# Pairs of 64-column stationaries in one attention head of a float32 kernel

## The chip, the cores and the metric

The kernel runs on one core of one Trainium2 chip. The metric is the device time of one execution in microseconds (us); less is better. Engines carry the names of the profile: PE is the matrix engine (PEld is its loading of stationary operands, which has a row of its own), DVE the vector engine, ACT the scalar engine, POOL the GpSimd engine, SP the engine that mostly issues transfers.

## The reference

The input is one sequence of 2048 rows of 256 numbers, all float32. It is normalized, and the same normalized rows go into an attention with 16 heads of 128 and into a feed-forward part with quantized weights; both results are added to the input.

```python
xn = _layernorm(x)                                  # x: (1, 2048, 256)
q, k, v = split(einsum('bsd,ed->bse', xn, Wqkv))    # 16 heads of 128
logits = einsum('bqhd,bkhd->bhqk', q, k) * 128 ** -0.5
w = softmax(logits, axis=-1)
out = einsum('bhqk,bkhd->bqhd', w, v)               # (1, 2048, 16 * 128)
attn = einsum('bse,de->bsd', out, Wout)
ffn = bitlinear(sigmoid(bitlinear(xn, w1)) * bitlinear(xn, w2), w3)
return x + attn + ffn
```

## The kernel before, in words

After a start of about 110 us (normalization, the first head's q, k and v, the feed-forward part) the kernel goes through the attention head by head. A head's 2048 query rows are four blocks of 512 (`b` 0 to 3), and all 64 blocks are numbered through: block `n` is head `n // 4`, so head 2 is blocks 8 to 11. A block is four steps (`t` 0 to 3) of 128 queries. The order of instructions is written out by hand (`tc.manual_schedule()`): each engine takes them in the order in which the main loop records them. The loop runs over steps `u`, and in each step it records, for PE,

- `scores(v)` for a step six ahead (`v = u + LEAD`): the logits of 128 queries against all 2048 keys, as two tiles `s` of 128 queries by 1024 keys, four matmuls in all. A matmul's stationary operand is a 128 x 128 piece of `qT`, its moving operand 512 columns of `kT`. DVE takes each tile's row maximum (line 617), ACT the exponential (line 627).
- one or two products for the next head's q, k and v, or for the output projection (`pw` line 166, `pvw` line 280, `pow` line 783), placed before and among the weighted sums.
- four calls of `weighted(n, k)` (line 690), `k` being one of 16 groups of 128 keys: the stationary operand is a 128 x 128 piece of `v`, the moving operand the 512 columns of the turned exponentials `pT`, and the sum over `k` grows in one tile `av` (128 x 512). After `k` 15 DVE multiplies it by the reciprocal sums (line 701).

Between the two, `exchanged(v)` sends the exponentials through 16 transfers (line 646, queues of SP and ACT) into `part`, and `transposed` (line 680, DVE) turns them in pieces of 32 x 32 into `pT`. So keys reach PE as the summed dimension without a product on PE.

A float32 `matmul` of the program is two passes on PE: the profile shows two loads of the stationary operand and two MATMUL records for each. A record writes its operands as `128*128`, the rows and columns of the array that it uses, and the shape of the moving operand.

Which array columns a matmul uses follows from the program: a stationary operand of 64 columns uses half of them, and which half is set by the partitions of its output, 0 to 63 or 64 to 127.

The loop's body, where the pieces are put in order, is this:

```python
if more:
    scores(v, late=beside)          # `beside` records the first product
...
if u >= 0:
    for k in range(t * KQ, t * KQ + ahead):
        weighted(n, k)
if twice:
    pms.append(product(*hi, True))  # the second product
...
if u >= 0:
    for k in range(t * KQ + ahead, (t + 1) * KQ):
        weighted(n, k)
```

Of the kernel before, what the change touches and what calls it, by code (L numbers as in the profile page):

```python
# [19 lines left out]
def layernorm_attention_bitffn_kernel(  # L20
# [14 lines left out]
    nc = tc.nc  # L35
    P = 128
# [6 lines left out]
    QB = 512  # L43
    NB = S // QB
    TB = QB // P
    NKT = S // P
    KQ = NKT // TB
    HALF = S // 2
# [45 lines left out]
    kTs, qTs, vs = {}, {}, {}  # L94
# [142 lines left out]
    def v_tile(h: int):  # L237

        if h == 1:
            return osums.rearrange("p b e (k d) -> p (b e k) d", d=D)  # L240
        if h not in vs:
            vs[h] = kvpool.tile([P, NKT, D], F32, tag="v", name=f"v{h}", bufs=3)
        return vs[h]

    def v_place(h: int, k: int):


        return (k + NKT // 2) % NKT if h == 1 else k
# [344 lines left out]

    NQ = P // 32
    SP_DMAS = 10

    blocks = [(h, b) for h in range(H) for b in range(NB)]
    sums, exps, parts, pTs, avs, rbs = {}, {}, {}, {}, {}, {}

    def scores(v: int, late=None):  # L600

        n, t = divmod(v, TB)
        h, b = blocks[n]
        halves, ps = [], []
        mx = small.tile([P, 2], F32, tag="mx", name=f"mx{v}")
        for i in range(2):
            s = ps_s.tile([P, HALF], F32, tag="s", name=f"s{v}_{i}")  # L610
            for j in range(HALF // QB):
                nc.tensor.matmul(  # L612
                    s[:, bass.ts(j, QB)], qTs[h, b][:, bass.ts(t, P)],
                    kTs[h][:, i * HALF + j * QB : i * HALF + (j + 1) * QB],
                    start=True, stop=True,
                )
            nc.vector.tensor_reduce(mx[:, i : i + 1], s, AX.X, ALU.max)  # L617
            halves.append(s)
        nm = small.tile([P, 1], F32, tag="nm", name=f"nm{v}")
        nc.vector.tensor_reduce(nm, mx, AX.X, ALU.max, negate=True)  # L620
        if t == 0:
            sums[n] = small.tile([P, TB, 2], F32, tag="sum", name=f"sum{n}")
        if late:
            late()
        for i, s in enumerate(halves):
            p = ppool.tile([P, HALF], F32, tag="p", name=f"p{v}_{i}", bufs=4)
            nc.scalar.activation(  # L627
                p, s, AF.Exp, bias=nm, accum_out=sums[n][:, t, i : i + 1],
            )
            ps.append(p)  # L630
        exps[v] = ps

    def exchanged(v: int):
# [7 lines left out]
        for m, (j, g) in enumerate(todo):  # L641
            queue = nc.sync if m < SP_DMAS else nc.scalar
            if v > len(blocks) * TB - 3:
# [38 lines left out]
    def weighted(n: int, k: int, part=None):  # L682

        h, b = blocks[n]
        t0, t1 = (0, TB) if part is None else (part * TB // 2, (part + 1) * TB // 2)
        if k == 0:
            pool, tag = (ps_s, "s") if part == 0 else (ps_av, "av")
            avs[n] = pool.tile([P, QB], F32, tag=tag, name=f"av{n}_{t0}")
        av = avs[n][:, : (t1 - t0) * P]
        nc.tensor.matmul(  # L690
            av, v_tile(h)[:, v_place(h, k), :],
            pTs[n][:, t0:t1].rearrange("p t g (k q) -> p (t g) k q", q=32)[:, :, k, :],
            start=(k == 0), stop=(k == NKT - 1),
        )
        if k == NKT - 1:

            m = 1 if part == 1 else t1 - t0
            for t in range(t0, t1, m):
                o, a = oT[:, t * P : (t + m) * P], av[:, (t - t0) * P : (t - t0 + m) * P]
                if n < NBK - NB:  # L700
                    nc.vector.tensor_tensor(o, a, rbs[n][:, t * P : (t + m) * P], ALU.mult)  # L701
                else:
                    nc.vector.tensor_copy(o, a)
# [228 lines left out]
    with tc.manual_schedule():  # L932
        for u in range(-LEAD, (NBK - 1) * TB):
            n, t = divmod(u, TB)
# [3 lines left out]
            h, b = blocks[v // TB] if more else (H, 0)  # L938
# [7 lines left out]
            g, i = divmod(n, GB)  # L946
            if n >= NB and t < 2:
                i, j = divmod(i, NB)
                j = 2 * j + t
# [17 lines left out]
            if more:  # L967
                scores(v, late=beside)
# [28 lines left out]
# [3 lines that stand above are left out]
# [13 lines left out]
# [3 lines that stand above are left out]
# [10 lines left out]
        n = NBK - 1  # L1026
        for k in range(NKT):
            weighted(n, k, 0)
            if k in (KQ - 1, 3 * KQ - 1):
                projected(n - 1, k // (2 * KQ), ps_s, "s")  # L1030
            elif k == 2 * KQ - 1:
                opened(NB - 1, 0, ps_s, "s")
# [44 lines left out]
```

## Time and profile before

| what | value |
|---|---|
| time, median of 3 runs | 2243.17 us (2242.22 to 2247.93) |
| profiled execution, from first to last instruction | 2242.2 us |
| the same execution's time outside that span | not given; its span lies within 0.1 us of the fastest run's time |
| granted PE clock, whole span | 1.000 |
| PE busy | 2230.5 us, 5434 passes |
| DVE, ACT, POOL busy | 1772.0, 652.4, 681.1 us |
| scores (line 612) | 2048 passes, 922.5 us busy |
| weighted sums (line 690) | 2080 passes, 947.9 us busy in two groups |

The page gives busy time per engine over the span, and groups of instructions by line, operand names and shape, each with its count, busy time and the mean duration of one. A pass's duration in the records is longer than the distance to the next one, since a pass starts before the one ahead of it has left the array; the distance from start to start says what a pass costs in a row of passes. The time line lists instructions in order: start and length in us, engine, line, operation, and in brackets how long the engine was idle before and what ended that.

### The profile page before, as it was taken

What the parts mean: (1) busy time and instruction counts of PE and PEld (TensorE: products, weight loads), DVE (VectorE), ACT (ScalarE), POOL (GpSimd) and SP (SyncE); (2) the same over time, 40 slices, a digit from 0 to 9 for tenths busy, and PEclk for the clock granted to TensorE, in tenths of its full rate; (3) what the DMA queues carried; (4) which work ended last, traced back from release to release, by engine and by line L of the source; (5) the groups of instructions that cost most, each with busy time, mean ns of one, the idle gap of its engine ahead of it and who ended that gap; (6) DMA issues with size and microseconds to landing.
All of it is one profiled execution on the core that took longest, in us unless ns stands there. A gap on an engine that the chain in (4) does not pass through costs nothing.

```text
span 2242.2 us, 24572 instructions
## 1 busy us (share of the span) xinstructions
PE 2230.5 (99%) x5434; PEld 1025.3 (46%) x5434; DVE 1772.0 (79%) x2329; ACT 652.4 (29%) x1138; POOL 681.1 (30%) x1223
## 2 busy tenths in 40 slices
PE   9999999999999999999999999999999999999999
PEld 6744444444444444444444444444444444444445
DVE  6577778888788878888788878788778887888876
ACT  5543222222222222222222222222222222222231
POOL 0021144231452223522234313332134221452442
PEclk9999999999999999999999999999999999999999
DMA  2166666775676666676666766667566676676775
GB/s 91 50 161 172 156 166 172 186 195 157 165 196 179 185 159 164 188 203 169 155 176 179 197 179 150 176 181 199 163 166 179 175 197 159 158 200 181 197 202 145
DMA packets 252515, 382.72 MB, mean 171 GB/s; under 512 B 86224, under 2 KB 90768, under 8 KB 252368
## 3 DMA queue, kind: packets, MB, share of 16 engines
q1 hardware_dynamic: 127664, 174.95, 30.3%
q10 hardware_dynamic: 74896, 101.94, 17.2%
q0 software_dynamic: 49808, 104.27, 16.6%
q8 instruction: 43, 0.70, 0.1%
q14 instruction: 104, 0.85, 0.1%
HBM read 62.98 MB, written 34.73 MB: 44 GB/s over the span
## 4 chain that ended last, share of the span: by engine, by line
PE 67%; DMA 16%; DVE 7%; SPq 5%; issue 2%; ACTq 2%; ACT 1%; DVEq 0%; POOL 0%
PE s L612 26%; PE av L690 25%; DMA part<-p 16%; PE pw L166 5%; SPq L646 5%; DVE pT L680 3%; PE pvw L280 3%; PE pow L783 3%; PE ph L495 2%; ACTq L646 2%; DVE mx L617 1%; PE pf L518 1%; ACT p L627 1%; DVE osums L790 1%; PE pv L229 1%
## 5 line engine op out<-in xcount | busy, mean ns | idle before, releaser
L627 ACT ACTIVATE p<-s,nm 128x1024 f32<-128x1024 f32 x512 | 566.1, 1110 | 1512.5 <-DMA part<-p 1269.5
L612 PE MATMUL s<-kT,qT 128*128 128x512 f32 x2048 | 922.5, 593 | 2.6 <-ACT p L627 2.4
L617 DVE TENSOR_REDUCE mx<-s 128x1 f32<-128x1024 f32 x512 | 623.6, 1221 | 353.5 <-PE s L612 353.3
L690 PE MATMUL av<-pT,v 128*128 128x512 f32 (+1 forms) x1952 | 888.4, 585 | 0.0
L680 DVE STREAM_TRANSPOSE pT<-part 128x1024 f32<-128x1024 f32 x512 | 605.2, 1220 | 37.3 <-DMA part<-p 31.1
L612 PEld LDWEIGHTS s<-kT,qT 128*128 128x128 f32 x2048 | 388.3, 190 | 493.6 <-issue 474.7
L690 PEld LDWEIGHTS av<-pT,v 128*128 128x128 f32 x1952 | 370.9, 190 | 450.2 <-issue 448.0
L665 POOL DMA_DIRECT2D rd<-r x240 | 124.9, 527 | 616.8 <-DVE r L663 614.0
L311 POOL DMA_DIRECT2D xnT<-v x448 | 221.1, 501 | 84.9 <-DVE v L304 54.4
L723 POOL TENSOR_TENSOR o<-o 128x512 f32<-128x512 f32 x56 | 71.2, 1271 | 198.6 <-PE pow L783 168.4
L708 POOL DMA_DIRECT2D od<-oT x60 | 34.1, 568 | 300.5 <-DVE oT L701 300.5
L790 DVE TENSOR_TENSOR osums<-pow,osums 128x512 f32<-128x512 f32 x196 | 124.2, 675 | 0.0
L627 ACT ACTIVATION_READ_ACCUMULATOR p<-s,nm 128x1 f32 x512 | 100.3, 196 | 0.0
L166 PE MATMUL pw<-t,ws 128*128 128x512 f32 x168 | 86.6, 597 | 1.0 <-DVE kT L193 1.0
L189 DVE TENSOR_TENSOR kT<-pw,kT 128x512 f32<-128x512 f32 x112 | 74.7, 667 | 0.0
L304 DVE TENSOR_TENSOR v<-pvw,v 128x512 f32<-128x512 f32 x98 | 65.5, 680 | 0.1
L690 PE MATMUL av<-pT,osums 128*128 128x512 f32 x128 | 59.5, 592 | 0.0
L186 DVE SCALAR_TENSOR_TENSOR qT<-pw,qT 128x512 f32<-128x512 f32 x84 | 57.5, 684 | 0.1
L166 PE MATMUL pw<-xnT,wk 128*128 128x512 f32 x112 | 57.2, 592 | 0.0
L783 PE MATMUL pow<-o,wos 128*128 128x512 f32 x112 | 57.2, 592 | 0.0
L166 PEld LDWEIGHTS pw<-t,ws 128*128 128x128 f32 x168 | 31.0, 189 | 44.1 <-issue 34.0
L620 DVE TENSOR_REDUCE nm<-mx 128x1 f32<-128x2 f32 x256 | 39.7, 155 | 13.4
(140 smaller groups left out, 1146.6 us busy)
## 6 DMA issues: line engine op xcount, KB each, us to landing
part<-p SPq DMA_DIRECT2D x2556, 64.0 KB, 2.2
part<-p ACTq DMA_DIRECT2D x1540, 64.0 KB, 2.5
oT<-rd POOLq DMA_DIRECT2D x60, 256.0 KB, 4.1
od<-oT POOLq DMA_DIRECT2D x60, 256.0 KB, 3.3
o<-od POOLq DMA_DIRECT2D x60, 256.0 KB, 4.5
xnT<-v POOLq DMA_DIRECT2D x448, 32.0 KB, 2.4
osums<-yd POOLq DMA_DIRECT2D x28, 512.0 KB, 5.4
yd<-osums POOLq DMA_DIRECT2D x28, 512.0 KB, 4.7
```

The source lines that it names most:

```text
L166: nc.tensor.matmul(pm, lhs, rhs, start=True, stop=True)
L189: nc.vector.tensor_tensor(k, pk, base, ALU.add)
L311: nc.gpsimd.dma_start(v_part[q // 2][bass.ts(j, 32), bass.ts(q % 2, S // 8)], v[bass.ts(q, 32), bass.ts(j, S // 8)],)
L612: nc.tensor.matmul(s[:, bass.ts(j, QB)], qTs[h, b][:, bass.ts(t, P)], kTs[h][:, i * HALF + j * QB : i * HALF + (j + 1) * QB], start=True, ...
L617: nc.vector.tensor_reduce(mx[:, i : i + 1], s, AX.X, ALU.max)
L627: nc.scalar.activation(p, s, AF.Exp, bias=nm, accum_out=sums[n][:, t, i : i + 1],)
L646: queue.dma_start(parts[v][g // 2][bass.ts(j, 32), g % 2, :], ps[j // 2][bass.ts(g, 32), bass.ts(j % 2, S // NQ)],)
L665: nc.gpsimd.dma_start(rds[n % 2][:, bass.ts(j, 32)], riT[32 * j : 32 * j + TB, :])
L680: nc.vector.transpose(pTs[n][:, t, 2 * i : 2 * i + 2], part)
L690: nc.tensor.matmul(av, v_tile(h)[:, v_place(h, k), :], pTs[n][:, t0:t1].rearrange("p t g (k q) -> p (t g) k q", q=32)[:, :, k, :], start=( ...
L783: nc.tensor.matmul(pm, lhs, o3[:, i], start=True, stop=True)
L790: nc.vector.tensor_tensor(y, pm, y, ALU.add)
```

## The change

In head 2 every weighted sum is done with stationary operands of 64 columns instead of 128, in pairs: one works on the left half of the array's columns and writes partitions 0 to 63 of `av`, the other on the right half and writes partitions 64 to 127. In blocks 8 and 10 (`b` 0 and 2) both of a pair go over the same 512 moving columns. In blocks 9 and 11 (`b` 1 and 3) each matmul is cut again into two of 256 moving columns, recorded in the order left half with columns 0 to 255, right half with 256 to 511, left with 256 to 511, right with 0 to 255. In blocks 10 and 11 the scores are made in pairs in the same way, each of 64 queries against 512 keys. What is computed, the tiles and all other engines' instructions stay the same, and so does the order of the work around it; all other heads are untouched.

```diff
+    HALVED = 2
...
             for j in range(HALF // QB):
-                nc.tensor.matmul(
-                    s[:, bass.ts(j, QB)], qTs[h, b][:, bass.ts(t, P)],
-                    kTs[h][:, i * HALF + j * QB : i * HALF + (j + 1) * QB],
-                    start=True, stop=True,
-                )
+                m = P // 2 if h == HALVED and b > 1 else P
+                for a in range(0, P, m):
+                    nc.tensor.matmul(
+                        s[a : a + m, bass.ts(j, QB)], qTs[h, b][:, t * P + a : t * P + a + m],
+                        kTs[h][:, i * HALF + j * QB : i * HALF + (j + 1) * QB],
+                        start=True, stop=True,
+                    )
...
-        nc.tensor.matmul(
-            av, v_tile(h)[:, v_place(h, k), :],
-            pTs[n][:, t0:t1].rearrange("p t g (k q) -> p (t g) k q", q=32)[:, :, k, :],
-            start=(k == 0), stop=(k == NKT - 1),
-        )
+        vk = v_tile(h)[:, v_place(h, k), :]
+        pk = pTs[n][:, t0:t1].rearrange("p t g (k q) -> p (t g) k q", q=32)[:, :, k, :]
+        if h == HALVED:
+            m, w = P // 2, QB // (1 + b % 2)
+            for i in range(QB // w):
+                for j in range(2):
+                    q = i ^ (j if w < QB else 0)
+                    nc.tensor.matmul(
+                        av[j * m : (j + 1) * m, bass.ts(q, w)], vk[:, bass.ts(j, m)],
+                        pk[:, q * w // 32 : (q + 1) * w // 32],
+                        start=(k == 0 and i == 0), stop=(k == NKT - 1), skip_group_check=True,
+                    )
+        else:
+            nc.tensor.matmul(av, vk, pk, start=(k == 0), stop=(k == NKT - 1))
```

## The prediction, made before the changed kernel was run

> **What bounds the kernel now.** I first read the page's busy times and slices: PE is busy through all 40 slices at the full granted clock.
>
> ```profile
> PE 2230.5 (99%) x5434; PEld 1025.3 (46%) x5434; DVE 1772.0 (79%) x2329; ACT 652.4 (29%) x1138; POOL 681.1 (30%) x1223
> PE   9999999999999999999999999999999999999999
> PEclk9999999999999999999999999999999999999999
> ```
>
> Busy is not yet full use, so the windows view comes next, over head 2's four blocks. Eight blocks of 32 weighted-sum passes are done by 394.4 us, and the next 128 passes fill 394.4 to 529.4 us.
>
> ```profile
> 394.40:529.40 135.00, 134.86 (x313) 58.85 (x312) 111.03 (x145) 36.82 (x64) 36.11 (x59) 1.00 0.71 189
> ```
>
> The columns after the length are PE, PEld, DVE, ACT and POOL. PE is idle for 0.14 us, and the waits view has no wait of PE in this window. Everything else has room, DVE least: 111.0 of 135.0 us. How far apart passes start is in the chain that ended last, in order of time:
>
> ```profile
> 410.28 0.86 PE pw L166 x2
> 411.14 1.72 PE av L690 x4
> ...
> 415.64 3.43 PE s L612 x8
> ```
>
> Eight passes take 3.43 us, so one of 128 x 512 costs 0.429 us, and 312 of them are 133.8 of the 135.0 us. PE's passes alone set the end here: whatever they gain or lose is the kernel's.
>
> **What the change touches.** Weighted sums: 4 blocks x 16 groups = 64 matmuls, 128 passes. Scores: blocks 10 and 11, 8 steps x 4 = 32 matmuls, 64 passes. Together 192 passes x 0.429 = 82.4 us. Afterwards blocks 8 and 10 have 128 weighted passes of 64 columns x 512, blocks 9 and 11 have 256 of 64 x 256, and the scores 128 of 64 x 512.
>
> **The price if halves do not overlap.** A pass is priced by its moving columns. The time line at the kernel's end shows 256 of them per pass:
>
> ```profile
> 2226.70 3.43 PEld L690 LDWEIGHTS av<-pT,v 128*128 128x128 f32 x16
> 2230.15 0.84 PEld L836 LDWEIGHTS pp<-wo,o 128*128 128x128 f32 x4
> ```
>
> 16 passes to the next group are 3.45 us, 0.2156 each; half the moving columns is half the price. Nothing says that half the array columns would be cheaper in sequence. So the sequence costs 256 x 0.429 + 256 x 0.2156 = 165.0 us in place of 82.4, 82.6 more.
>
> **The price if they overlap.** Two passes of one matmul use the same half and can't run beside each other; the second pass of the left matmul can run beside the first of the right, the right's second beside the next left's first. A run of n pairs then takes 2n + 1 pass times instead of 2n: one pass more per run. In the built order the 64-column work stands in 28 runs, cut by the products (`pw`, `pow`) and by full scores; 18 end in passes of 512, 10 in passes of 256. 18 x 0.429 + 10 x 0.2156 = 9.9 us.
>
> **Changing over.** Before and after each run, PE goes from whole-width work to half-width and back, 56 times. No pass of before uses half the columns, but the feed-forward part has the mirror case: its last group uses 64 rows of the array. PE's time line there, and that of the loads:
>
> ```profile
> 56.05 0.61 PE L495 MATMUL ph<-xh,w1q 128*128 128x512 f32 x2
> 56.59 0.50 PE L518 MATMUL pf<-hidl,w2q 64*128 64x512 f32 x1
> 56.93 0.39 PE L518 MATMUL pf<-hidh,w2q 64*128 64x512 f32 x1
> ...
> 57.40 0.39 PE L518 MATMUL pf<-hidh,w2q 64*128 64x512 f32 x1
> 57.72 0.73 PE L495 MATMUL ph<-xl,w0q 128*128 128x512 f32 x2
> 58.29 0.62 PE L495 MATMUL ph<-xh,w0q 128*128 128x512 f32 x2
> ```
>
> ```profile
> 56.59 0.18 PEld L518 LDWEIGHTS pf<-hidl,w2q 64*128 64x128 f32 x1 [0.35 <-issue]
> 56.70 0.19 PEld L518 LDWEIGHTS pf<-hidh,w2q 64*128 64x128 f32 x1
> ```
>
> Normally these one-pass products start 0.23 us apart, and the next load starts with the pass ahead of it. The last whole-height pass starts at 56.05 + 0.23 = 56.28; the next load comes only at 56.59, 0.08 after the streaming should have ended, and then lies open itself (0.11 us from one load's start to the next). From that pass to the second of the new kind it is 0.65 us for two steps of 0.23: 0.2 us lost. Back again, 57.40 to 58.29 is 0.89 for three: 0.2 us too. So 56 x 0.20 = 11.2 us; a 64-column load may be half as long, 56 x 0.15 = 8.4. I take 11.2, the measured one.
>
> [...]
>
> **Loads.** Now a load lies under the pass ahead of it, and PE's row has 0.24 us left over each time. In pairs there are two loads per 0.429 us, or, in blocks 9 and 11, two per 0.2156 us; at 0.11 us from load to load for full stationaries both fit, the second barely. So I take nothing. If the order of the queue leaves two loads of 0.107 us open per pair (0.107 is the finer reading of the 0.11 above), the 128 matmul pairs (32 + 64 + 32) cost 128 x 2 x 0.107 = 27.4 us more. I keep both ends.
>
> [...]
>
> **Other engines.** No instruction of DVE, ACT, POOL or SP changes. A score tile that comes late delays its maximum and exponential, but scores run six steps (some 50 us) ahead of the sums that use them, so PE doesn't wait for that; ACT already waits 88 of the 135 us for transfers of `part`, and a slower PE shortens that wait. The next thing to be late would be DVE, 24 us away, in a direction that a longer PE only widens.
>
> **The sum.** Forecast, halves overlap: 9.9 + 11.2 = +21.1 us, 2242.2 -> 2263.3 on the profiled execution. Its span lies 1.0 us under the median of the runs, so 2264. This case's own range: 2251 (cheaper changeovers, no single pass left over at the ends) to 2292 (loads open).
>
> **Rivals.** *Serial:* the halves take turns, since PE takes passes in order and a float32 pass may hold the whole array. +82.6 + 11.2 = +93.8, 2337. For it: no row of before shows two passes side by side; records overlap only by the 0.16 us by which 0.593 exceeds 0.429. Against it: a load already works beside a pass, so the array is not one resource.
>
> *Not slower:* the halves overlap from the first pass, and the column split needs no changeover. Both terms go, 2243. It decides if a change costs under 0.05 us and left and right first passes start together; against it stands that two passes of one matmul stand between them in the queue, and that the row split pays 0.20 us eight times out of eight.
>
> *Faster:* half-width float32 passes run at the pace of the feed-forward's one-pass products, 0.227 in place of 0.429 us, and overlap too: 192 x 0.202 = -38.8 + 21.1, so 2226. Only a pass priced by its width as well would do this; 256 against 512 columns shows pricing by moving columns alone.
>
> **How the numbers follow.** A measurement of this kernel can tell about 0.3% (6.7 us) from no change. Forecast 0.56, serial 0.32, not slower 0.08, faster 0.04. The predicted time is the forecast's 2264. Its own range leaves out over 2 in 10, so mine must reach the serial case: 2250 to 2341, the top allowing for a few loads left open in series. Slower by over 0.3% (above 2249.9) gathers forecast and serial, 0.88; within, 0.08; faster, 0.04.
>
> **What would show it.** In the profile after: 64-column MATMUL records on lines 700 and 615, each with a partner from the other half starting within some ns, and starts of one half 0.858 us apart per matmul pair of 512. If so the stretch that was 135.0 us is about 156; if starts follow each other at 0.429 without partners, it is about 229. Changeovers show as idle before a load of about 0.35 us and more. I am wrong if the stretch differs and PE's idle rises by waits for DVE or ACT, if 256-column blocks cost clearly more than 512-column ones (loads), or if the time leaves the range.

## The result, and the profile after

The changed kernel takes 2254.62 us, median of 4 runs (2253.6 to 2261.09), against 2245.39 us for the kernel before beside it (4 runs): a ratio of 1.0047, interval 1.0026 to 1.0068. The profiled execution's span went from 2242.2 to 2251.3 us, +9.1 us. That is slower and inside the range, but less than half of the +21.1 us that the prediction's sum gave.

The page after has PE just as busy as before, with 320 more passes (5754 instead of 5434):

```profile
PE 2239.8 (99%) x5754; PEld 1021.2 (45%) x5754; DVE 1772.0 (79%) x2329; ACT 651.9 (29%) x1138; POOL 679.1 (30%) x1223
PEclk9999999999999999999999999999999999999999
```

The groups by shape show the new passes; the last two numbers before the idle are busy us and mean ns of one:

```profile
L700 PE MATMUL av<-pT,v 128*64 128x256 f32 x256 | 30.7, 385 | 0.0
L700 PE MATMUL av<-pT,v 128*64 128x512 f32 x128 | 30.6, 603 | 0.0
L615 PE MATMUL s<-kT,qT 128*64 128x512 f32 x128 | 28.8, 592 | 0.0
```

128 passes of 512 columns in 30.6 us are 0.24 us each, and 256 of 256 columns 0.12 each: little more than half of what a pass costs alone (0.429 and 0.216). So they run two by two. The windows view of head 2, from its first weighted pass to the first of head 3 (in the order PE, PEld, DVE, ACT, POOL):

```profile
394.70:538.40 143.70, 143.70 (x634) 54.95 (x634) 111.24 (x145) 36.80 (x64) 35.61 (x58) 1.00 0.67 179
```

From start to start this stretch has grown from 135.13 to 143.72 us, +8.6 of the +9.1. DVE, ACT and POOL do what they did. PE is busy for all of it, so "busy" hides the loss; it is in the distances. PE's time line at the beginning of the stretch, start and length first:

```profile
393.72 1.02 PE L795 MATMUL pow<-o,wos 128*128 128x512 f32 x2
394.67 2.80 PE L700 MATMUL av<-pT,v 128*64 128x512 f32 x12
397.40 1.12 PE L795 MATMUL pow<-o,wos 128*128 128x512 f32 x2
398.46 1.08 PE L700 MATMUL av<-pT,v 128*64 128x512 f32 x4
```

Twelve half-width passes, the work of six whole ones, take 2.73 us to the next line's start; six whole ones would be 2.57. The loads of the same place show where the difference is:

```profile
393.72 0.19 PEld L795 LDWEIGHTS pow<-o,wos 128*128 128x128 f32 x1 [0.24 <-issue]
394.67 0.20 PEld L700 LDWEIGHTS av<-pT,v 128*64 128x64 f32 x4 [0.76 <-issue]
395.16 0.14 PEld L700 LDWEIGHTS av<-pT,v 128*64 128x64 f32 x2 [0.29 <-issue]
395.58 0.14 PEld L700 LDWEIGHTS av<-pT,v 128*64 128x64 f32 x2 [0.28 <-issue]
...
397.40 0.30 PEld L795 LDWEIGHTS pow<-o,wos 128*128 128x128 f32 x2 [0.81 <-issue]
398.45 0.20 PEld L700 LDWEIGHTS av<-pT,v 128*64 128x64 f32 x4 [0.76 <-issue]
```

Inside the stretch two loads start every 0.429 us (395.16, 395.58): one per half, and in the trace the two passes they serve start 0.007 us apart, first pass beside first, second beside second. (The records don't name the half. That the two belong to different halves follows from the program and the counts: passes of one half follow each other at 0.429 us.) At the borders loads wait: 0.76 us of idle at all 28 ways in; on the way out 0.81 after passes of 512 moving columns and 0.39 after those of 256. Idle of PEld alone is no price, since a load normally idles 0.24 us here; the price is in the starts of the passes. In start-to-start distances the trace has 28 changes into halves at 0.144 us each and 28 back at 0.204, each the same to within 0.003: 4.04 + 5.72 = 9.76 us.

### The profile page after: what moved, and what is told of

Same layout as the page of the kernel before. It is cut to its first block, busy times and chain, and to the rows that moved or that the text cites. A ratio compares the mean times of both kernels' runs of the same rounds, so it can differ in the third digit from the quotient of the medians.

```text
span 2251.3 us, 25213 instructions
## 1 busy us (share of the span) xinstructions
PE 2239.8 (99%) x5754; PEld 1021.2 (45%) x5754; DVE 1772.0 (79%) x2329; ACT 651.9 (29%) x1138; POOL 679.1 (30%) x1223
## 4 chain that ended last, share of the span: by engine, by line
PE 78%; DMA 11%; DVE 5%; SPq 3%; issue 1%; ACT 1%; ACTq 1%; DVEq 0%; POOL 0%
PE s L615 30%; PE av L706 28%; DMA part<-p 10%; PE pw L166 6%; PE pvw L280 3%; SPq L649 3%; PE pow L795 3%; PE av L700 3%; DVE pT L683 2%; PE ph L495 2%; DVE mx L620 1%; PE pf L518 1%; ACT p L630 1%; DVE osums L802 1%; ACTq L649 1%
## 5 line engine op out<-in xcount | busy, mean ns | idle before, releaser
L615 PE MATMUL s<-kT,qT 128*128 128x512 f32 (+1 forms) x2112 | 923.5, 593 | 1.8 <-ACT p L630 1.6
L706 PE MATMUL av<-pT,v 128*128 128x512 f32 (+1 forms) x1824 | 829.0, 585 | 0.0
L615 PEld LDWEIGHTS s<-kT,qT 128*128 128x128 f32 (+1 forms) x2112 | 384.8, 187 | 494.9 <-issue 478.0
L706 PEld LDWEIGHTS av<-pT,v 128*128 128x128 f32 x1824 | 346.6, 190 | 419.6 <-issue 417.3
L700 PE MATMUL av<-pT,v 128*64 128x256 f32 (+1 forms) x384 | 61.3, 457 | 0.0
```

Of the source, the lines that this page charges most:

```text
L615: nc.tensor.matmul(s[a : a + m, bass.ts(j, QB)], qTs[h, b][:, t * P + a : t * P + a + m], kTs[h][:, i * HALF + j * QB : i * HALF + (j + 1) ...
L700: nc.tensor.matmul(av[j * m : (j + 1) * m, bass.ts(q, w)], vk[:, bass.ts(j, m)], pk[:, q * w // 32 : (q + 1) * w // 32], start=(k == 0 and ...
L706: nc.tensor.matmul(av, vk, pk, start=(k == 0), stop=(k == NKT - 1))
```

## The experiments

**Everything in head 2 in pairs.** Products and all scores of the sixteen steps are halved as well, so PE changes over once each way.

```diff
-                m = P // 2 if h == HALVED and b > 1 else P
+                m = P // 2 if paired else P
...
+    def product_of(pm, lhs, rhs):
+        m = P // 2 if paired else P
+        for a in range(0, P, m):
+            nc.tensor.matmul(pm[a : a + m], lhs[:, a : a + m], rhs, start=True, stop=True)
...
+            paired = HALVED * NB * TB <= u < (HALVED + 1) * NB * TB
```

> All PE work of head 2's sixteen steps (weighted sums, scores, products) is done in 64-column pairs, so PE changes over once into pairs and once back, with 188 pairs in place of 96 (as the change has them, counted in whole matmuls). If only change-overs cost (0.144 us in, 0.204 us out, as the trace of the changed kernel has them): +0.35 us, no difference from before. If a half-width pass costs by itself (the change's 9.8 us over the 192 passes that it replaced, 0.05 each): 376 passes x 0.05 = +19 us.

Measured: 2244.21 us against 2243.39 (11 and 15 runs), ratio 1.0005, interval 0.9996 to 1.0014; span 2242.4 us. The stretch is back at 135.0 us, though it now holds 744 passes, nearly all of half width:

```profile
394.80:529.80 135.00, 134.82 (x744) 61.29 (x741) 111.17 (x145) 36.80 (x64) 36.07 (x59) 1.00 0.70 189
```

```profile
390.47 0.20 PEld L621 LDWEIGHTS s<-kT,qT 128*64 128x64 f32 x4 [0.76 <-ACT p L636]
390.96 0.14 PEld L621 LDWEIGHTS s<-kT,qT 128*64 128x64 f32 x2 [0.29 <-issue]
```

These loads are the only way in, with the 0.76 us of before a first load. (The 376 passes of the second reading count each 256-column pair as one of its own; counted in whole passes it is 312 x 0.05 = +16 us. The time moved by 0.8 us, so both counts are ruled out.) A pair of half-width passes costs no more than a whole one, within the interval; the change's price is in its borders.

**Weighted sums alone.** The change without its halved scores (`m = P` in `scores`).

> The change without its halved scores: 128 whole passes replaced in place of 192, in the same 28 stretches. If change-overs are the cost: 28 x 0.348 = +9.7 us, as with the whole change. If passes are: 128 x 0.05 = +6.5 us.

Measured: 2254.16 us against 2243.39, ratio 1.0046, interval 1.0032 to 1.006; the stretch is 143.72 us, to the hundredth as with the whole change. A third of the replaced passes less, the same 28 borders, the same time. 6.5 us (1.0029) lies just outside the interval, and the stretch rules it out.

**The sides in turn.** In each group of weighted sums first all left halves, then all right ones.

```diff
-                for k in range(t * KQ, t * KQ + ahead):
-                    weighted(n, k)
+                for side in (0, 1) if blocks[n][0] == HALVED else (None,):
+                    for k in range(t * KQ, t * KQ + ahead):
+                        weighted(n, k, side=side)
```

(The second group of a step likewise; moving columns are 512 throughout, scores whole.)

> Weighted sums of head 2 in halves of 512 moving columns, but in each group of one to four keys' tiles first all left halves are issued, then all right ones (14 groups of 3, 14 of 1, 4 of 2); scores whole. If each side of the array goes through its own passes whatever was issued between: +9.7 us, change-overs alone. If PE takes passes in the order of issue and only neighbours run side by side: a group of n takes 2n - 1 matmul times of 0.858 us in place of n, 32 more in all: +27.5 + 9.7 = +37 us. If nothing overlaps any more: +55 + 9.7 = +65 us.

Measured: 2263.15 us, one run, span 2261.4, the stretch 156.30 us: +21.2. None of the three readings holds. The loads of a group of three:

```profile
394.03 0.19 PEld L697 LDWEIGHTS av<-pT,v 128*64 128x64 f32 x2 [0.76 <-issue]
394.51 0.14 PEld L697 LDWEIGHTS av<-pT,v 128*64 128x64 f32 x1 [0.29 <-issue]
394.94 0.19 PEld L697 LDWEIGHTS av<-pT,v 128*64 128x64 f32 x3 [0.29 <-issue]
395.37 0.19 PEld L697 LDWEIGHTS av<-pT,v 128*64 128x64 f32 x2 [0.23 <-issue]
395.80 0.19 PEld L697 LDWEIGHTS av<-pT,v 128*64 128x64 f32 x2 [0.23 <-issue]
396.28 0.14 PEld L697 LDWEIGHTS av<-pT,v 128*64 128x64 f32 x1 [0.29 <-issue]
396.71 0.14 PEld L697 LDWEIGHTS av<-pT,v 128*64 128x64 f32 x1 [0.29 <-issue]
```

The left side runs alone at first (one load at a time); at 394.94 three loads come at once, by the counts one of the left and two of the right: the first right pass starts two passes after the left began, with three left passes ahead of it in the order still to start. From there both sides run beside each other until the left is done. Each of the 14 groups of three loses one matmul time this way, 14 x 0.858 = 12.0 us, and 0.057 us more where its left side ends, 0.8 us in all. With 9.7 us of change-overs, less the 1.2 us of late loads that this stretch had before, that is 21.3 of the measured 21.2. Groups of two lose nothing, their right side starts 0.013 us after the left, there too with three left passes ahead of it still to start. So in this run a right pass started ahead of three left passes that come before it in the order, and not ahead of five or four (at 394.03 and 394.51 no right pass started).

**Sides in groups of four.** The same with longer groups, to see whether it is three again. The second product moves behind all four keys' tiles.

```diff
+            if 0 <= u and blocks[n][0] == HALVED:
+                ahead = KQ
```

> As the run with the sides in turn, but each of head 2's sixteen steps does its four keys' tiles in one group: four left halves, then four right ones; 16 stretches of pairs in place of 28. If PE looks over at most three waiting passes, as there (a right half was let in when three passes of the left were still ahead of it): the right side begins with the third left matmul, two matmul times of 0.858 us lost in each group, 16 x 1.716 = 27.5 us, and 16 x 0.348 = 5.6 us of change-overs: the stretch of head 2 from 135.1 to about 168 us. If instead a long group always loses just one matmul time: 13.7 + 5.6, about 154.5 us. If groups of four end all overlap: 16 x 3 x 0.858 + 5.6, about 182 us.

Measured: 2278.14 us, one run, span 2276.3, the stretch 167.65 us, where 168 was expected. The right side comes in with the third left matmul (398.09; the five loads before it are all of the left side):

```profile
396.32 0.19 PEld L697 LDWEIGHTS av<-pT,v 128*64 128x64 f32 x2 [0.76 <-issue]
396.81 0.14 PEld L697 LDWEIGHTS av<-pT,v 128*64 128x64 f32 x1 [0.29 <-issue]
397.23 0.14 PEld L697 LDWEIGHTS av<-pT,v 128*64 128x64 f32 x1 [0.29 <-issue]
397.66 0.14 PEld L697 LDWEIGHTS av<-pT,v 128*64 128x64 f32 x1 [0.29 <-issue]
398.09 0.19 PEld L697 LDWEIGHTS av<-pT,v 128*64 128x64 f32 x3 [0.29 <-issue]
```

Again three left passes ahead of the first right one were still to start; at the four starts before, with seven, six, five and four of them to come, no right pass started. (The 168 us left out two small things of opposite sign: the late loads of before, and 16 x 0.057 us where a left side ends.) What sets the three, these two runs don't show.

**Quarters.** Four stationaries of 32 columns in place of two of 64, in the weighted sums of head 2.

```diff
-            m, w = P // 2, QB // (1 + b % 2)
...
+            m = P // 4
+            for j in range(4):
+                nc.tensor.matmul(
+                    av[j * m : (j + 1) * m], vk[:, bass.ts(j, m)], pk,
+                    start=(k == 0), stop=(k == NKT - 1),
+                )
```

> Weighted sums of head 2 with stationaries of 32 columns, four to a matmul, on four quarters of the columns; scores whole. If quarters overlap like halves and the change-over into them has an open load of a quarter's length (0.092 + 0.026 us in, 0.204 out): 28 x 0.322 = +9.0 us. If only two run side by side: 64 x 0.858 + 9 = +64 us. The idle before the first load of a stretch should be the same as with halves, the first distance between passes shorter.

Measured: 2253.79 us, one run, span 2252.0, the stretch 143.19 us.

```profile
397.09 0.16 PEld L698 LDWEIGHTS av<-pT,v 128*32 128x32 f32 x8 [0.76 <-issue]
397.55 0.13 PEld L698 LDWEIGHTS av<-pT,v 128*32 128x32 f32 x4 [0.30 <-issue]
397.98 0.13 PEld L698 LDWEIGHTS av<-pT,v 128*32 128x32 f32 x4 [0.30 <-issue]
```

Four loads every 0.43 us: all four quarters run together. Their passes start within 0.020 us of each other, though three second passes stand ahead of the fourth quarter's first, in line with the three of the two runs above. The idle ahead is again 0.76 us, but the way in costs 0.118 us in the trace instead of 0.144. The way out, counted from the first of the passes that run side by side, is 0.218 us instead of 0.204; counted from the last of them it is 0.198 with halves and with quarters. So the distances have the same two parts at every change-over. The first pass starts 0.09 us later than one pass time after the last one (0.522 in place of 0.429 us after 512 moving columns, 0.309 in place of 0.216 after 256); the pass after it on the same columns is late once more, by 0.024 us where the stationaries that come have 32 columns, 0.05 for 64 and 0.104 for 128. That this second part is a load with no pass beside it is an estimate, from the 0.055 us (64 columns) and 0.109 us (128) from load to load at the borders of the changed kernel; what PE does in the first part, no record shows.

**All heads.** The weighted sums of all blocks but the last in halves (`if part is None` in place of `if h == HALVED`, 512 moving columns).

> Weighted sums of all blocks but the last in pairs of 64 columns over the same 512 moving columns; scores whole. 419 stretches of pairs. If change-overs are the cost: 419 x 0.348 = +145.8 us, 2389 us (6.5% slower). If a half-width pass costs by itself, 0.05 us for each of 2016 replaced: +101 us. If the late loads of before vanish under the change-overs as in head 2, some us less.

Measured: 2382.12 us against 2242.8, ratio 1.0625, interval 1.0609 to 1.0641; span 2378.3 us, +136.1. The trace has 419 changes each way at 0.144 and 0.204 us, 146 us together. What is missing from the +146 was there before: between 110 and 2190 us the passes of the kernel before start late by 10.0 us in all (distances over 0.429 us added up, late loads for a product or a score tile). Here passes that are late elsewhere than at a border come to 0.2 us, and 146 - 10.0 is the 136 that was measured.

**Whole rows in the feed-forward part.** The kernel before, with the last group's operands made up to 128 rows by zeros, so that the row split from which the prediction took its price disappears.

```diff
+        if p0:
+            for o in hid:
+                nc.gpsimd.memset(o[:p0].bitcast(F32), 0.0)
...
-                    yTs[c][e], quantized[2][p0:, f, bass.ts(e, P)], hid[i][p0:],
+                    yTs[c][e], quantized[2][:, f, bass.ts(e, P)], hid[i],
```

> The kernel before, with the feed-forward's last group of 64 rows made up to 128 rows: the other 64 rows of both operands are zeros (POOL sets those of the moving operand), so PE never changes to 64 rows. If the 0.20 us lost at each of the 8 changes to 64 rows and back is the change-over: the feed-forward stretch 1.6 us shorter, 0.07% of the time, which the times can hardly tell. If it is a wait for the values (DVE, ACT), the late loads stay and nothing is gained.

Measured: 2242.81 us against 2242.8 (11 and 15 runs), ratio 1.0001, interval 0.9992 to 1.001. The feed-forward stretch went from 70.11 to 69.27 us, -0.84, half of what was expected. The loads behind the last group now follow without a gap, but the next chunk's first sums wait for something else:

```profile
58.61 0.41 PEld L495 LDWEIGHTS ph<-xl,w0q 128*128 128x128 f32 x2
...
60.70 0.19 PEld L521 LDWEIGHTS pf<-hidl,w2q 128*128 128x128 f32 x1 [0.31 <-ACT yT L528]
...
61.18 0.19 PEld L521 LDWEIGHTS pf<-hidl,w2q 128*128 128x128 f32 x1 [0.19 <-ACT yT L528]
```

The change-over is real, all eight are gone. But the eighth lies behind the last product, where the stretch as measured ends, so 1.43 us could be gained in it; and PE, now earlier, meets ACT's copy of the last sums (line 528) three times and gives some 0.19 us back at each, 0.56 in all. 1.43 - 0.56 = 0.87 us is left, against the 0.84 measured.

## Why the prediction was right or wrong

**What bounds the kernel:** right. PE's passes alone set the time; with twice as many passes at the same total width (the first experiment) the time is the same, and with 419 borders it grows by their price.

**Overlap against taking turns:** right. The price without overlap, +82.6 us, would with the change-overs have put the stretch near 229 us; it is 143.7, and each pass has its partner 0.007 us away.

**One pass left over per run, 9.9 us:** this step failed, and it is the larger part of the miss. It assumed, with no row to show it, that a right matmul's first pass has to wait until the left one's second pass begins. The trace has the first passes side by side from the start, 0.007 us apart, and the runs with the sides in turn agree: there a right pass started with three left passes ahead of it still to start (at 394.94 and 398.09). In the change's order only one stands between. The term is 0. (The sign that the prediction named for its overlap, a stretch of about 156 us, is missed for the same reason.)

**Change-overs, 11.2 us:** right in kind, a little too dear: 9.76 us. The row split's 0.20 us was the right row for the way out (0.204); on the way in, where the loads have 64 columns, the price is 0.144. The prediction named that shorter load, but as one price for both ways, 0.15, and took the longer one for both; the trace has a price for each way.

**Loads, nothing:** right. In blocks 9 and 11 the pairs start 0.216 us apart, as whole passes of 256 columns do. Inside the stretch the loads of both halves lie beside running passes (two loads at 395.16, with two passes of 0.592 us that began at 395.15 and 395.16), and two halves, and four quarters, overlap whole: their passes start within 0.007 and 0.020 us of each other.

**What the sum left out:** the stretch before had 1.2 us of late starts at five loads, two for scores that waited for ACT and three for products, of which one waited for DVE and two for nothing that the profile shows. One of these two:

```profile
439.60 0.30 PEld L783 LDWEIGHTS pow<-o,wo 128*128 128x128 f32 x2 [0.76 <-issue]
```

So idle of 0.76 us isn't by itself the mark of a change-over: a late load does it too, and the pass after it is late once more, by 0.075 to 0.105 us at these five. In the changed kernel no start in the stretch is late except at a border, presumably because PE comes to these places later, or at a change-over; no run tells the two apart. So 9.76 - 1.2 = 8.5 us is left, against 8.6 measured in the stretch and 9.1 over the span. In all heads the same effect is 10.0 us.

**Rivals:** *not slower* had its first condition right (both sides start together) and its second wrong; its point, 0.05 us a change, lies well under the 0.174 us of the mean one. *Serial* and *faster* are ruled out by the distances.

**The number:** the time lies inside the range, but near its lower end. The range was made wide to reach the serial case, so that says little for the forecast; its own lower bound, 2251, is for cheaper change-overs and no single pass left over, and that is the case that came.

## What to carry to other kernels

Half-width stationaries in pairs cost nothing in themselves here and bring nothing either (everything in head 2 in pairs: ratio 1.0005); the price is in going from whole to half width and back, 0.35 us a round trip in this float32 kernel. Count the borders in the built order, not the passes, and put all neighbours into the same split if one of them needs it. If halves are issued in turn, keep partners close: here a right pass started with three left passes ahead of it still to start, and none with four, and each float32 matmul on one side beyond two cost one matmul time, 0.858 us.

And read "busy" as no more than that: PE was busy for 143.70 of 143.70 us while it lost 9.8.

## What the runs showed of the hardware that was not expected

- The two halves, and the four quarters, start their passes close together though a float32 matmul's second pass stands between them in the order: 0.007 us apart in the changed kernel, 0.020 from the first quarter to the fourth. With everything in pairs most partners start 0.036 us apart, and that costs nothing either. In both runs with the sides in turn a right pass started with three left passes ahead of it still to start, and none did with four.
- A load of 64 columns is in the records for 0.136 us and one of 128 for 0.190, but where two loads of a side follow each other at once, as at the borders, it is 0.055 and 0.109 us from one start to the next.
- A stall that was taken away and a stall that was added did not add up here: late loads of 10.0 us shrank to 0.2 with the 838 change-overs of all heads, and 0.56 of the 1.43 us that seven row changes cost came back as waits for ACT.
